# Other tie rules for TensorE in a list scheduler, with the ranks searched anew

## The chip, the cores and the metric

The kernel runs on one core of one Trainium2 chip. The metric is the device time of one execution in microseconds; several executions are timed and the median is given.

## The reference, cut to what matters

32 sequences of 256 tokens with 256 features pass through four layers, all in float32:

```python
out = silu(scale * layer_norm(x) + shift) @ W_in + b_in          # layer 0, norm over the whole sequence
x   = silu(scale * layer_norm(out) + shift) @ W_out + b_out + x
x   = ln(x) * (1 + scale) + shift                                 # layer 1: attention with a bias and a mask
s   = q @ k.T / sqrt(16) + attention_bias                         # 16 heads of 16
x   = x + softmax(where(mask, -inf, s)) @ v @ Wo + bo
x   = x + gelu2((ln(x) * g2 + beta2) @ W1 + b1) @ W2 + b2         # 256 -> 1024 -> 256
x   = max(x + dt * (stencils of x), 0)                            # layer 2: gradients along both axes
h   = layer_norm(x)                                               # layer 3: causal attention, exact gelu
x1  = x + softmax(causal(q @ k.T / sqrt(16))) @ v @ Wo + bo
x2  = x1 + gelu(layer_norm(x1) @ W1 + b1) @ W2 + b2
return x + g * (x2 - x)
```

The batches do not depend on each other; within a batch each layer needs the one before.

## The kernel before, in words

The kernel does not issue its instructions as the program text has them. Every engine is wrapped by a recorder (`Order.engine`, `Order.record`), which notes each operation with its operands, an estimate of its length and its dependences. The three generators `layer_0`, `layer_1` and `layers_23` describe one batch each. The function `trace` runs through a generator and gives each of its steps a rank, which is a wished-for time: batch times `PERIOD`, plus the layer's `START`, plus an `EDGE` for single early and late batches, plus a `SHIFT` for single steps. `PACE` stretches a layer's steps. So several batches lie on top of each other: while layer 3 of one batch runs, layer 1 of the next and layer 0 of a later one run between its operations.

`Order.arrange` then walks through time as a list scheduler. Whenever an engine is free by its own book-keeping, it takes from the operations that are ready the one with the lowest rank. `Order.emit` issues everything in the order of the start times found (line 382 is the one call through which all of it passes, so nearly all rows of the profile name L382; one tells groups apart by their tiles). The order on each engine is thus fixed when the program is built. On the chip the engines run it in order and wait for each other by semaphores.

A TensorE unit is a group of matmuls recorded together. There are three array shapes:

- scores (tile `sc`): 32 rows by 128 columns, four heads beside each other, out of `k_t` and `nq0` or `nq1`;
- values (tile `mm`, out of `pt` and `L1v` or `L3v`): 128 rows by 32 columns;
- everything else is full-size, 128 by 128. It is of two kinds: transposes (tiles `tr`, and `mm` with `ident`), which take one pass, and float32 matmuls, which take two passes. The profile counts passes.

In attention, a scores group of four heads goes to VectorE, which adds the bias and finds the minimum (`pr`, `mn`), then to ScalarE, which takes the exponential in place (`pr`). TensorE transposes the result (`tr`), VectorE and ScalarE copy it to SBUF in turns (`pt`), and the values follow. `wide`, the inverse sums spread by GpSimd, is transposed too and multiplied in. The feed-forward tiles are `h_t`, `L1w` or `L3w` and `hid`; the stencil's are `gd`, `b0f` and `rows_t`; normed rows are `t`.

PSUM has eight banks, all of one tag. `CAPS` says how many of them scores (`sc`), transposed probabilities (`tr`) and other results (`mm`) may hold at once. `EARLIER` lets these kinds go ahead of their rank by so much.

What the change is about stands in the choice of TensorE's next unit, in `arrange`:

```python
if e == "pe" and units[u][2][0]["length"][1] != shape:
    rank += self.STAY
    if units[u][2][0]["length"][1] != (P, P):
        rank -= self.PAIR if shape != (P, P) else 0.0
    elif units[u][2][0]["length"][3] == 2:
        rank += self.FRESH
```

`shape` is the shape that the array has now. A unit of another shape has its rank raised by `STAY` (5.0). If the array has a small shape and the candidate has the other small one, `PAIR` is taken off. If the candidate is a full-size matmul of two passes, `FRESH` is put on; a full-size transpose (one pass) gets neither. Ranks are in the scheduler's own microseconds.

The DMA loads (`nb`, a quarter of a megabyte of attention bias each, `x`, `mask`) are all issued from SyncE's queue in an order that the same scheduler sets.

Of the kernel before, what the change touches and what calls it, by code (L numbers as in the profile page):

```python
# [38 lines left out]

PERIOD = 86.0
START = (-61.8, 0.0, 116.9)
PACE = (1.55, 1.23, 1.08)
EDGE = {(0, 0): 14.4, (0, 1): -5.0, (0, 2): 5.8, (1, 0): -19.0, (1, 1): -3.8, (1, 2): -0.2, (2, 0): -27.1, (2, 1): -2.0, (2, 2): -1.1, (3, 0): 12.3, (3, 1): 0.4, (3, 2): 0.3, (4, 0): 5.2, (4, 1): 2.3, (4, 2): 0.6, (27, 0): -1.1, (27, 1): -1.0, (27, 2): 0.5, (28, 0): 1.7, (28, 1): -0.3, (28, 2): -2.0, (29, 0): 2.1, (29, 1): -0.1, (29, 2): -2.1, (30, 0): -11.1, (30, 1): 5.7, (30, 2): -4.5, (31, 0): -16.9, (31, 1): 1.9, (31, 2): 15.4}
SHIFT = (
    {0: -93.0, 1: -33.6, 2: -27.5, 3: -32.8, 4: -14.7, 5: -56.4, 6: -42.3, 7: -28.3, 8: 23.1},
    {0: -9.7, 1: -80.2, 2: -10.3, 3: -1.7, 4: 2.7, 5: 8.8, 7: -7.0, 8: 14.7, 9: -90.2, 11: 7.3,
     12: 21.2, 13: -0.4, 14: 4.0, 15: -1.3, 16: 11.4, 17: 5.1, 19: 4.8, 20: 10.4, 21: 46.1, 22: 16.4,
     23: -8.7, 24: -13.1, 25: -30.4, 26: -2.4, 27: -90.0, 28: 8.3, 29: -134.0, 30: -0.4, 31: -13.2,  # L50
     32: -34.6, 33: 0.8, 34: -0.3, 35: 7.7, 36: -2.9, 37: -8.0},
    {0: -1.1, 1: -32.9, 2: -9.3, 3: 27.2, 4: 23.9, 5: -25.6, 6: -48.6, 7: -36.4, 8: -12.9, 9: 6.6,
     11: 3.0, 12: 15.4, 13: -32.5, 15: -6.5, 16: 20.0, 17: -2.0, 18: 6.6, 19: -0.5, 20: 0.4, 21: -82.2,
     23: 9.0, 24: 7.5, 25: 0.1, 26: -11.0, 27: -38.3, 28: 12.2, 29: 7.0, 30: 30.4, 31: 3.6, 32: -8.7,
     33: -46.1, 34: 4.4, 35: 2.3, 36: -58.5, 37: -16.3, 38: -59.7, 39: 18.0, 40: -15.2, 41: 12.6},
    {0: -24.5, 1: -13.3, 2: 6.7, 3: -84.2, 4: 42.8},
)
NORM = 8.0
LAND = 3.0
# [5 lines left out]
class Order:  # L65
# [13 lines left out]
    APART = 120.0  # L79
    SLACK = 50.0  # L80
    SEEN = {(32, P): 165.0, (P, 32): -16.0, (P, P): 165.0}
    CAPS = {"sc": 8, "tr": 7, "mm": 7}
    EARLIER = {"sc": 29.6, "mm": -2.0, "tr": 6.2}
    STAY = 5.0
    FRESH = 1.0
    PAIR = 0.0
    PORT = 0.05
    TABLES = {AF.Sin: 0, AF.Tanh: 1, AF.Exp: 1, AF.Gelu: 2}
    TABLE = 1300.0
# [127 lines left out]
    def arrange(self):  # L217
# [5 lines left out]
        turns = defaultdict(list)  # L223
        room = dict(self.CAPS)
        first = {}
        for u, (engine, rank, xs) in enumerate(units):
# [6 lines left out]
            for t in {t.name: t for x in xs for t in x["tiles"]}.values():  # L233
                f = first.setdefault(t.name, u)
                if f == u:
                    room[t.tag] = t.bufs or t.tag_meta.bufs
                    count[t.tag] += 1
                    if t.source_name in self.CAPS:
                        count[t.source_name] += 1
# [10 lines left out]
        for u, (engine, rank, xs) in enumerate(units):  # L250
            name = next((t.source_name for x in xs for t in x["tiles"] if t.source_name in self.CAPS), "")
            ranks.append((rank - (self.EARLIER.get(name, 0.0) if engine == "pe" else 0.0), u))
        for us in turns.values():
# [27 lines left out]
        while todo:  # L281
# [6 lines left out]
            for e in self.ENGINES:  # L288
# [6 lines left out]
                for k, heap in ready[e].items():  # L295
# [5 lines left out]
# [6 lines that stand above are left out]
                    if k[1]:  # L307
# [123 lines left out]
def kernel(ctx: ExitStack, tc: tile.TileContext, io, out, n_batch=B):  # L431
# [89 lines left out]
    def turned_vectors(tag, names, eng):  # L521
        vectors, n_rows = {}, 0
        for name in names:
            n = io[name].shape[0] // P
            vectors[name] = slice(n_rows, n_rows + n)
            n_rows += n
        as_rows = sb.tile([n_rows, P], F32, tag="nq0", name="as_rows")
        for name, at in vectors.items():
            eng.dma_start(as_rows[at], io[name].rearrange("(c p) -> c p", p=P))
        pm = mm_tile([P, n_rows])  # L530
        pe.transpose(pm, as_rows, ident[0:n_rows, 0:n_rows])
        cols = ctile(tag, [P, n_rows])
        dve.tensor_copy(cols, pm)
        return cols, {name: cols[:, at] for name, at in vectors.items()}
# [116 lines left out]
    sync.dma_start(parity, io["c_parity"])  # L651
    order.now = START[0] + 5.0
    _, more = turned_vectors(
# [501 lines left out]
    def trace(n, gen, layer, start, pace):  # L1155
        i = 0
        while True:
            order.now = start + SHIFT[layer].get(i, 0.0)
            step = next(gen, None)
            if step is None:  # L1160
                break
            start += step * pace
            i += 1

    trace(3 * n_batch, loads(), 3, START[1] + 25.0, 1.0)
    res = {}
    for b in range(n_batch):
        for i, layer in enumerate((layer_0, layer_1, layers_23)):
            trace(3 * b + i, layer(b, res), i, b * PERIOD + START[i] + EDGE.get((b, i), 0.0), PACE[i])
    with tc.manual_schedule():  # L1170
# [34 lines left out]
```

## Time and profile before

| | us |
|---|---|
| median of 3 runs (2664.05 to 2667.85) | 2665.15 |
| the profiled execution, its own time | 2665.54 |
| its span, first to last instruction | 2663.7 |
| TensorE busy | 2600.2 |
| VectorE busy | 2122.1 |
| ScalarE busy | 1920.1 |
| GpSimd busy | 1565.0 |

The profile was taken in one execution; its span is 1.8 us shorter than its time. A TensorE row's duration reaches from its start to its modelled end, and one overlaps the next, so what a matmul occupies is read from its start to the start of the next. Rows of the timeline are merged: the first column is the start of the first instruction, the second the time to the end of the last, and x8 is the number of passes. In the rows of the waits, the numbers are the microseconds in total, how often, and the longest. The row PEclk is the clock that TensorE was granted, in tenths of full speed, in 40 equal slices of the span.

### The profile page before, as it was taken

The page shows a single profiled execution, that of the slowest core. Times are in us where ns is not written, and L with a number is a line of the kernel's source. Part 1 is how long each engine was busy: PE and PEld are TensorE (multiplying, and loading weights), DVE is VectorE, ACT ScalarE, POOL GpSimd, SP SyncE. Part 2 cuts the span into 40 slices and gives each one's busy share as a digit, 9 for nine tenths or more (in the row PEclk, how much of TensorE's full clock was granted, in tenths as well). Part 3 has the DMA queues.
Part 4 walks back from the last instruction along what each step waited for, and adds up shares of the span by engine and source line. Part 5 has one row for each costly group of instructions (what it writes and reads, how often), then busy time and mean ns, then how long its engine had stood idle before and what let it go on. Part 6 is the DMA issues. An engine that isn't in the chain of part 4 may idle for free.

```text
span 2663.7 us, 60400 instructions
## 1 busy us (share of the span) xinstructions
PE 2600.2 (98%) x20462; PEld 2118.4 (80%) x20462; DVE 2122.1 (80%) x7627; ACT 1920.1 (72%) x6120; POOL 1565.0 (59%) x1960
## 2 busy tenths in 40 slices
PE   5999999999999999999999999999999999999997
PEld 4777888888888888888888888888888888888775
DVE  5887888878878877878878878877878887887853
ACT  2677777877777877777777777877777877777854
POOL 3865676555676555576555677555576555676420
PEclk7999999999999999999999999999999999999998
DMA  7321122212122212122212122212122211122100
GB/s 243 110 60 59 42 73 69 70 49 66 45 70 70 70 49 66 46 70 69 70 49 65 43 73 70 69 49 66 46 69 69 70 57 57 42 69 64 45 5 9
DMA packets 177064, 169.69 MB, mean 64 GB/s; under 512 B 19514, under 2 KB 175220, under 8 KB 176756
## 3 DMA queue, kind: packets, MB, share of 16 engines
q1 hardware_dynamic: 176720, 165.82, 20.2%
q8 instruction: 163, 2.67, 0.4%
q14 instruction: 145, 1.19, 0.1%
q10 hardware_dynamic: 36, 0.01, 0.0%
HBM read 157.40 MB, written 8.39 MB: 62 GB/s over the span
## 4 chain that ended last, share of the span: by engine, by line
PE 91%; DVE 3%; ACT 2%; DMA 1%; POOL 1%; issue 1%; SPq 0%; ACTq 0%; POOLq 0%; DVEq 0%
PE mm L382 68%; PE tr L382 14%; PE sc L382 9%; DVE pr L382 1%; ACT hid L382 1%; ACT pr L382 1%; DMA x<-in_x_dram 1%; POOL nb L382 0%; DMA nb<-in_fside_Bx16xSxS_dram 0%; DVE pt L382 0%; ACT L382 0%; POOL rstd L382 0%; DVE gd L382 0%; DMA L1wo<-in_L_cond_Wo_dram 0%; DVE st L382 0%
## 5 line engine op out<-in xcount | busy, mean ns | idle before, releaser
L382 ACT ACTIVATE pr<-pr,mn 128x256 f32<-128x256 f32 (+1 forms) x2048 | 966.9, 478 | 93.0 <-DVE mn L382 91.8
L382 POOL TENSOR_TENSOR nb<-mask_f,nb 128x512 f32<-128x512 f32 x512 | 693.3, 1378 | 114.7 <-DMA nb<-in_fside_Bx16xSxS_dram 101.9
L382 PE MATMUL tr<-ident,pr 128*128 128x128 f32 x3584 | 508.5, 276 | 5.4 <-ACT pr L382 1.8
L382 PEld LDWEIGHTS tr<-ident,pr 128*128 128x128 f32 x3584 | 419.5, 143 | 85.8 <-ACT pr L382 29.1
L382 DVE CUSTOM_DVE_ANT_0 pr<-sc,nb 128x256 f32<-128x256 f32 x1024 | 388.0, 414 | 25.3 <-POOL nb L382 14.0
L382 ACT ACTIVATION_READ_ACCUMULATOR pr<-pr,mn 128x1 f32 x2048 | 398.0, 194 | 0.0
L382 DVE COPY pt<-tr 128x512 f32<-128x512 f32 (+1 forms) x512 | 311.3, 615 | 72.9 <-PE tr L382 72.3
L382 POOL TENSOR_SCALAR hid<-hid 128x256 f32<-128x256 f32 x256 | 100.0, 405 | 433.4 <-ACT hid L382 433.1
L382 DVE CUSTOM_DVE_ANT_0 pr<-sc,causal 128x128 f32<-128x128 f32 (+1 forms) x1024 | 299.3, 352 | 38.5 <-PE sc L382 37.2
L382 PE MATMUL sc<-k_t,nq 32*128 32x256 f32 (+1 forms) x4096 | 269.5, 375 | 0.1
L382 ACT COPY pt<-tr 128x512 f32<-128x512 f32 (+1 forms) x512 | 261.4, 526 | 10.9 <-PE tr L382 6.0
L382 PE MATMUL mm<-L3w,hid 128*128 128x256 f32 x1024 | 241.5, 385 | 10.1 <-ACT hid L382 10.0
L382 PE MATMUL mm<-h_t,L3w 128*128 128x256 f32 x1024 | 247.6, 382 | 1.5 <-DVE h_t L382 1.4
L382 PE MATMUL mm<-h_t,L1w 128*128 128x256 f32 x1024 | 248.9, 381 | 0.0
L382 PE MATMUL mm<-L1w,hid 128*128 128x256 f32 x1024 | 239.0, 380 | 0.1
L382 PEld LDWEIGHTS sc<-k_t,nq 32*128 32x128 f32 x4096 | 163.3, 185 | 73.0 <-issue 25.7
L382 PEld LDWEIGHTS mm<-L3w,hid 128*128 128x128 f32 x1024 | 190.6, 193 | 35.1 <-ACT hid L382 11.9
L382 POOL COPY wide<-rs 128x256 f32<-128x256 f32 x128 | 53.3, 416 | 281.3 <-DVE rs L382 131.8
L382 PEld LDWEIGHTS mm<-L1w,hid 128*128 128x128 f32 x1024 | 186.6, 190 | 23.3 <-issue 1.2
L382 PEld LDWEIGHTS mm<-h_t,L3w 128*128 128x128 f32 x1024 | 184.2, 191 | 22.9 <-DVE h_t L382 2.5
L382 PEld LDWEIGHTS mm<-h_t,L1w 128*128 128x128 f32 x1024 | 183.7, 190 | 23.3 <-issue 1.8
L382 ACT ACTIVATE t<-x,shift,rstd 128x256 f32<-128x256 f32 x128 | 67.2, 590 | 148.8 <-DVE shift L382 148.8
(173 smaller groups left out, 4997.7 us busy)
## 6 DMA issues: line engine op xcount, KB each, us to landing
nb<-in_fside_Bx16xSxS_dram SPq DMA_DIRECT2D x512, 256.0 KB
x<-in_x_dram SPq DMA_DIRECT2D x32, 256.0 KB
out_dram<-d SPq DMA_DIRECT2D x32, 256.0 KB
mask<-in_mask_Bx1xSxS_bk_dram SPq DMA_DIRECT2D x32, 64.0 KB
L1w<-in_L_cond_W_dram SPq DMA_DIRECT2D x2, 1024.0 KB
L3w<-in_L_cond_W_dram SPq DMA_DIRECT2D x2, 1024.0 KB
l0w<-in_L_cond_W_dram SPq DMA_DIRECT2D x1, 1024.0 KB
g_b<-in_L_cond_B_grid_dram SPq DMA_DIRECT2D x3, 256.0 KB
```

The source lines that it names most:

```text
L382: call(*args, **kwargs)
```

## The change

Only constants change. `FRESH` goes from 1.0 to 16.0, and `PAIR` from 0.0 to 2.0. So behind a small shape a transpose goes ahead of a two-pass matmul unless its rank is 16 later, and a small group of the other shape is favoured by 2 among those that change the shape. Two bank caps move by one: `tr` may hold 8 and `mm` 6. The tables of ranks were searched together with these values, so they differ nearly everywhere, for the first and last batches most. Since the order of every engine follows from the scheduler, all engines' orders change somewhat, and SyncE's loads too; the instructions themselves are the same.

```diff
-PERIOD = 86.0
-START = (-61.8, 0.0, 116.9)
-PACE = (1.55, 1.23, 1.08)
-EDGE = {(0, 0): 14.4, (0, 1): -5.0, (0, 2): 5.8, (1, 0): -19.0, ...
+PERIOD = 85.9
+START = (-61.4, 0.0, 116.2)
+PACE = (1.47, 1.23, 1.08)
+EDGE = {(0, 0): -157.4, (0, 1): -5.7, (0, 2): 1.4, (1, 0): -49.3, ...
...
-    CAPS = {"sc": 8, "tr": 7, "mm": 7}
-    EARLIER = {"sc": 29.6, "mm": -2.0, "tr": 6.2}
+    CAPS = {"sc": 8, "tr": 8, "mm": 6}
+    EARLIER = {"sc": 28.0, "mm": -3.0, "tr": 6.3}
     STAY = 5.0
-    FRESH = 1.0
-    PAIR = 0.0
+    FRESH = 16.0
+    PAIR = 2.0
```

The entries of `SHIFT`, one per step of a layer, are replaced in the same manner.

## The prediction

> **What bounds the kernel now.** I read the page's busy shares first, then its chain, then TensorE's waits, then the timeline.
>
> ```profile
> PE 2600.2 (98%) x20462; PEld 2118.4 (80%) x20462; DVE 2122.1 (80%) x7627; ACT 1920.1 (72%) x6120; POOL 1565.0 (59%) x1960
> ...
> PEclk7999999999999999999999999999999999999998
> ...
> PE 91%; DVE 3%; ACT 2%; DMA 1%; POOL 1%; issue 1%; SPq 0%; ACTq 0%; POOLq 0%; DVEq 0%
> ```
>
> TensorE is busy for 98% of the span and is 91% of the chain; its clock is full in all but the first and last slices. Only TensorE's own work, and its 63.5 us of idle time (2663.7 - 2600.2), can change the end. TensorE's timeline puts 34.2 us of that idle in the first 100 us, 17.5 us after 2500 us, 5.6 us behind the last matmul, and nearly none between: two waits of 1.0 us, at 1320 and 1401. The chain repeats every 79.7 us per batch. So the middle is pure TensorE work, and what a TensorE instruction occupies there counts in full.
>
> What a change of tile shape costs is in TensorE's timeline. Columns: start, duration, what, how many passes.
>
> ```profile
> 1346.59 1.89 PE L382 MATMUL mm<-h_t,L3wk 128*128 128x256 f32 x8
> 1348.32 1.03 PE L382 MATMUL mm<-L3wv,h_t 128*128 128x256 f32 x4
> 1349.27 0.94 PE L382 MATMUL sc<-k_t,nq 32*128 32x128 f32 x16
> 1350.14 1.13 PE L382 MATMUL mm<-L3wv,h_t 128*128 128x256 f32 x4
> 1351.20 0.94 PE L382 MATMUL sc<-k_t,nq 32*128 32x128 f32 x16
> 1352.07 0.66 PE L382 MATMUL mm<-ident,t 128*128 128x128 f32 x4
> 1352.56 0.49 PE L382 MATMUL tr<-ident,pr 128*128 128x128 f32 x3
> ...
> 1366.05 1.15 PE L382 MATMUL sc<-k_t,nq 32*128 32x256 f32 x16
> 1367.13 1.51 PE L382 MATMUL mm<-pt,L3v 128*32 128x256 f32 x32
> 1368.57 0.87 PE L382 MATMUL tr<-ident,pr 128*128 128x128 f32 x6
> ...
> 1375.71 2.35 PE L382 MATMUL tr<-ident,pr 128*128 128x128 f32 x20
> 1377.89 3.62 PE L382 MATMUL mm<-L1w,hid 128*128 128x256 f32 x16
> ```
>
> Read from start to start. Eight full-size passes take 1.73 us, 0.216 each. The four at 1348.32, with scores next, take 0.95, not 0.86: **entering** a small shape costs 0.09. The four at 1350.14 lie between two score groups and take 1.06: **leaving into a matmul** costs 0.10 more. The four transposes at 1352.07 take 0.49 against 4 x 0.109: **leaving into a transpose** costs 0.056. Scores followed directly by values take 1.08, as before anything else, and the values take 1.44, as they do behind a full-size one: **small directly behind small** pays no entry. Medians over the trace: entry 93.5 ns, exit to a matmul 104 ns, exit to a transpose 56 ns.
>
> **The change part by part.** No instruction is added or removed: both orders hold 12606 TensorE instructions. The constants move only ranks, so I counted the boundaries in the two built orders.
>
> - Entries into a small shape from a full-size one: 327 before, 305 after. 22 x 93.5 ns = 2.06 us less.
> - Exits into a two-pass matmul: 96 to 46. 50 x 104 ns = 5.20 us less.
> - Exits into a transpose: 229 to 256. 27 x 56 ns = 1.51 us more.
> - Sum: 5.7 us less TensorE work. In one steady batch it is one entry less, two matmul exits less and one transpose exit more: 0.25 us of 79.7, 22 times (5.4 us). As a check, slots by kind plus these costs give 79.42 us per batch before; the trace has 79.71.
>
> **What could eat it in the middle.** Moving a group brings its operands due earlier or later. Links from TensorE through other engines back to TensorE keep their room in the steady batch: scores to transposes at least 4.5 us apart (3.3 before). Shorter are the last transpose before an L3 values group, 2.37 us ahead instead of the 2.94 that the trace ran without a wait (a pt copy takes 0.53 to 0.62, and the transpose's result about 0.27 more), rows_t to the norm's transposes (12.1 from 14.3; the chain needs 7.6, below) and layer 0's output to its norm (8.6 from 10.2). I charge nothing: 0 from one side; from the other 0.5 us per batch, 11 us. On POOL one nb subtraction (1.38 us) now stands between the two rstd steps behind the output projection, but that link grows from 7.86 to 8.73. SyncE's queue has the same loads in a batch, one nb load earlier past the mask; nb loads are covered, since DMA is busy a fifth of the time.
>
> **The tail.** Here the order changes most. After the last pass of layer 1's feed-forward, before has 51.3 us of work in a chain of 88.7 (2575.0 to 2663.7); after has 56.5 us. The 5.3 us more that lie inside the chain come off what precedes it. How long is the chain then?
>
> ```profile
> 2585.23 0.60 PE L382 MATMUL mm<-ident,rows_t 128*128 128x128 f32 x4
> 2589.55 8.26 PE L382 MATMUL mm<-L3w,hid 128*128 128x256 f32 x24 [3.71 <-ACT hid L382]
> 2597.64 0.60 PE L382 MATMUL mm<-ident,t 128*128 128x128 f32 x4
> ```
>
> The last batch's t was ready at 2593.4 (ScalarE's timeline), but its transposes queued until 2597.64 behind 24 passes of the batch before, at half clock after the 3.7 us idle. After, those transposes come directly behind rows_t: 4.2 us sooner, and 1.2 sooner ahead of them (four matmuls gone, stencil less late). The price: 7.6 us idle with nothing to fill it, so the 20 passes of Q, K and V (4.3 us) run partly at half clock, 3.3 us more. The previous batch's first feed-forward, 6.9 us, now lies in pieces between the attention's transposes: before took 26.9 us for 15.3 us of such work, after has 22.6 us in it; I add 1.5. Its second one fills the 3.7 us idle behind the last output projection, delays t by 1.5, but keeps the clock (FF1 took 8.73 instead of 6.9): zero. Sum -0.6, so the tail is worth 5.9 at best; the terms are estimates of 2 to 3 us each, and I take **4**, between 9 and -4.
>
> **The head.** Batch 1's layer 0 (l_win, two mean matmuls) now goes ahead of batch 0's Q. From before's rows that puts Q some 2.2 us later than 52.0, but takes about 2 us of TensorE and 5 us of VectorE work out of the attention behind it, where before idles 7 us and has one more half-clock stretch. I take 0.5 us gained, between 5 and -4.
>
> **Sum.** 2663.7 - 5.7 - 4 - 0.5 = 2653.5; with the 1.8 us around the span 2655.3 against the profiled execution's 2665.54, which lies 0.4 above the median of the runs (2665.15). I give 2655.
>
> **A rule that speaks against it.** The Trainium skill, "TensorE: Matmul & The Clock Gate", Part 4 (PE-mode transpose), says that a transpose takes about 275 ns in a kernel and does not count as activity for the clock in the way a matmul does. Transposes first would then make duller stretches behind small tiles: one window of the page's 3.4 us at half clock in a batch costs 1.7 us, 37 us over 22 batches. The trace disagrees: 20 transposes in a row at 1375.71 start 109 ns apart (their 276 ns is duration, overlapped), and the clock stays full through every such run in the middle. I go by the row.
>
> **Rivals.**
>
> *The ends give it back (chance 0.22).* The unfilled 7.6 us idle halves the clock for the whole attention behind it (as it did in stretches from 2616 to 2629), and the head's delay is not recovered: +6 on the forecast, 2661. For it: the clock did drop after every such idle. Against it: feed-forward matmuls now lie there.
>
> *Slower: VectorE loses the port (0.15).*
>
> ```profile
> 1238.20 0.68 DVE L382 TENSOR_TENSOR gd<-gd,a0f 128x512 f32<-128x512 f32 x1
> ...
> 1318.16 1.80 DVE L382 TENSOR_TENSOR gd<-gd,a0f 128x512 f32<-128x512 f32 x1
> ```
>
> The same instruction took 1.80 us when POOL's nb subtraction had started 0.01 us earlier (1318.15), and 0.68 when nb came later (1238.98). The stencil matmul then waited 1.0 us, and that batch lasted 80.98 us, not 79.71; so the next. It is a race of some 0.2 us, lost in 2 of 22 batches. The Trainium skill, "SBUF — State Buffer", Who interferes with whom, says that issue order decides and the loser blocks for the whole instruction: by it a small shift flips every batch, by the row 2 in 22. The new order keeps this place's sequence on TensorE, VectorE and POOL, so I keep 2. Lost in all, it costs 20 x 1.27 = 25 us: 2680. From 12 more lost batches the kernel is slower by over 0.2%.
>
> *The values' last copy is late (0.08).* 0.5 us per batch: 2666, no change.
>
> **How the numbers follow.** Forecast 0.55, with its own range 2648 to 2661. A measurement can tell about 0.2% from no change: 2659.8 to 2670.5 is "same". Faster: nearly all of the forecast and some of the first rival, 0.62; same 0.24; slower 0.14. The range for 8 in 10 takes the forecast's low end, the first rival and the copies' case: 2647 to 2668.
>
> **What would show it.** Right: boundaries in TensorE's timeline counted as above; a batch of about 79.45 us; no waits in the middle; busy TensorE some 6 us lower; t's transposes directly behind rows_t at the end after 7 to 8 us idle. Wrong: waits of 0.3 us or more repeated every batch in front of values or stencil (gd at 1.8 us), a clock below full in the middle slices, or from the last layer-1 feed-forward pass to the end much over 89 us.

## The result, and the profile after

| | before | after |
|---|---|---|
| median, us (20 runs each) | 2665.37 | 2669.17 |
| span of the profiled execution, us | 2663.7 | 2667.5 |
| up to batch 0's first L3wq matmul | 150.2 | 150.3 |
| batches 0 to 2 | 236.4 | 235.6 |
| batches 3 to 24, the 22 steady ones | 1756.7 | 1768.4 |
| the five behind them, 25 to 29 | 393.8 | 406.8 |
| the last two, to the end | 126.7 | 106.4 |

The ratio of after to before is 1.0014, with an interval of 1.0008 to 1.0021: slower by a little, where 2655 was forecast. (A batch is counted from its first L3wq matmul to that of the next.) The middle lost 11.7 us where 5.4 were to be gained; from batch 25 on it was 7.3 us faster.

First the page of after: busy time by engine, the granted clock, the chain by engine. (ScalarE's count has fallen by two: the program as it ran has 63 table loads, before had 65. All other instructions are the same in number.)

```profile
PE 2596.2 (97%) x20462; PEld 2123.4 (80%) x20462; DVE 2152.6 (81%) x7627; ACT 1927.2 (72%) x6118; POOL 1558.9 (58%) x1960
...
PEclk7999999999999999999999999999999999999999
...
PE 82%; ACT 7%; DVE 6%; POOL 2%; DMA 2%; issue 1%; SPq 0%; DVEq 0%; POOLq 0%; ACTq 0%
```

The clock is at nine tenths or more in all slices but the first, so no boundary has become dearer by the clock. But the chain that ended last lies on TensorE for 82% only, not 91%, and ScalarE has grown from 2% to 7%: TensorE waits for something more often. Its waits name it (total, how often, longest), first in after, then the same row in before:

```profile
PE tr L382 <- ACT pr L382: 13.7, 49, 1.2
```

```profile
PE tr L382 <- ACT pr L382: 1.8, 6, 0.5
```

The 6 waits have become 49, two in each steady batch. TensorE's timeline shows where, in a steady batch of after whose first L3wq matmul starts at 1109.56:

```profile
1117.62 0.94 PE L382 MATMUL sc<-k_t,nq 32*128 32x128 f32 x16
1118.49 0.55 PE L382 MATMUL tr<-ident,pr 128*128 128x128 f32 x3
1119.38 0.33 PE L382 MATMUL tr<-ident,pr 128*128 128x128 f32 x1 [0.35 <-ACT pr L382]
1119.88 0.77 PE L382 MATMUL tr<-ident,pr 128*128 128x128 f32 x5 [0.16 <-ACT pr L382]
1120.48 0.60 PE L382 MATMUL mm<-ident,t 128*128 128x128 f32 x4
```

Nine transposes directly behind layer 3's second scores group, as the new ties want it. They take 1.99 us from start to start (1118.49 to 1120.48) where nine in a row and one exit take 1.04: **0.95 us lost in each batch**. They wait for exponentials, so the next view is ScalarE's timeline of the same stretch, first in after:

```profile
1111.12 0.63 ACT L382 ACTIVATE th<-y 128x512 f32<-128x512 f32 x1 [2.52 <-DVE y L382]
1113.21 0.84 ACT L382 ACTIVATE k_t<-mm,cols 128x256 f32<-128x256 f32 x2 [1.46 <-PE mm L382]
1114.14 1.09 ACT L382 ACTIVATE t<-xm,shift,rstd 128x256 f32<-128x256 f32 x2
1115.25 1.28 ACT L382 ACT_TABLE_LOAD   x1
1116.55 0.40 ACT L382 ACTIVATE pr<-pr,mn 128x128 f32<-128x128 f32 x1
```

and in before (the batch starts at 1104.47):

```profile
1104.76 0.63 ACT L382 ACTIVATE th<-y 128x512 f32<-128x512 f32 x1 [1.24 <-DVE y L382]
1105.30 1.08 ACT L382 ACTIVATE t<-xm,shift,rstd 128x256 f32<-128x256 f32 x2
1108.12 0.84 ACT L382 ACTIVATE k_t<-mm,cols 128x256 f32<-128x256 f32 x2 [1.75 <-PE mm L382]
1108.98 1.28 ACT L382 ACT_TABLE_LOAD   x1
1110.28 0.40 ACT L382 ACTIVATE pr<-pr,mn 128x128 f32<-128x128 f32 x1
```

The same five rows stand in another order. `k_t` starts 3.65 us into the batch in both. In before, layer 1's second norm (`t<-xm`, 1.08 us) ran ahead of it, in time in which ScalarE idled. In after it stands behind it, between `k_t` and the first exponential, because the shift that it needs now lies behind `nq` in VectorE's queue. It came 0.17 us into the batch in before and comes 4.34 us into it in after (a row of each):

```profile
1104.64 0.33 DVE L382 TENSOR_SCALAR shift<-mv,rstd 128x1 f32<-128x1 f32 x2
```

```profile
1113.90 0.33 DVE L382 TENSOR_SCALAR shift<-mv,rstd 128x1 f32<-128x1 f32 x2
```

So the first exponential starts 6.99 us into the batch, not 5.81, and all those behind it are 1.2 us later. The table load, 1.28 us, is in that stretch in both.

### The profile page after: what moved, and what is told of

It reads as the page before. It is cut to its first block, busy times and chain, and to the rows that moved or that the text cites. A ratio compares the mean times of both kernels' runs of the same rounds, so it can differ in the third digit from the quotient of the medians.

```text
span 2667.5 us, 60293 instructions
## 1 busy us (share of the span) xinstructions
PE 2596.2 (97%) x20462; PEld 2123.4 (80%) x20462; DVE 2152.6 (81%) x7627; ACT 1927.2 (72%) x6118; POOL 1558.9 (58%) x1960
## 4 chain that ended last, share of the span: by engine, by line
PE 82%; ACT 7%; DVE 6%; POOL 2%; DMA 2%; issue 1%; SPq 0%; DVEq 0%; POOLq 0%; ACTq 0%
PE mm L382 61%; PE tr L382 14%; PE sc L382 7%; ACT pr L382 3%; DVE nq L382 2%; ACT L382 1%; ACT t L382 1%; POOL nb L382 1%; DVE pr L382 1%; DVE dd L382 1%; DMA nb<-in_fside_Bx16xSxS_dram 1%; DVE th L382 1%; DMA x<-in_x_dram 1%; ACT L3v L382 0%; ACT hid L382 0%
## 5 line engine op out<-in xcount | busy, mean ns | idle before, releaser
L382 PEld LDWEIGHTS tr<-ident,pr 128*128 128x128 f32 x3584 | 412.6, 142 | 110.3 <-ACT pr L382 40.4
L382 DVE COPY pt<-tr 128x384 f32<-128x384 f32 (+1 forms) x512 | 308.7, 613 | 28.6 <-PE tr L382 26.0
L382 PE MATMUL mm<-h_t,L1w 128*128 128x256 f32 x1024 | 244.3, 380 | 0.4 <-DVE h_t L382 0.4
L382 PE MATMUL mm<-h_t,L3w 128*128 128x256 f32 x1024 | 239.2, 380 | 0.6 <-DVE h_t L382 0.3
L382 DVE DVE_READ_ACCUMULATOR2_ANT mn<- 128x1 f32 x2048 | 167.9, 82 | 0.0
```

What stands on the lines that cost most here:

```text
L382: call(*args, **kwargs)
```

## The experiments

**Theory A**: what stands in ScalarE's queue between `k_t` and layer 3's first exponential sets the steady batch, through the exponentials that the nine transposes read; take 1 us of it away, and the 0.95 us go. **Rivals**: B, that TensorE's own order is at fault, which puts too little work between scores and transposes; C, that taking this wait away does not bring the time back, since it moves on; later D, that the strong tie puts the transposes too early whatever stands on ScalarE; and E, that each microsecond off that queue shortens the batch. All times below are medians of at least four runs, beside before on the same chip; spans and batches are from each kernel's profile.

### table_early: the table drawn forward

```diff
         for x in sorted(xs, key=lambda x: x["start"]):
+            if x.get("mark") == "k3":
+                early()
...
-        order.emit()
+        order.emit(lambda: nc.scalar.activation(spare, mhalf[:, 0:1], AF.Exp))
```

A one-column exponential of a constant is issued on ScalarE ahead of each layer-3 `k_t`. Nothing else moves.

> The changed kernel plus one exponential of a single column on ScalarE ahead of each layer-3 k_t, whose result nobody reads: the table load of 1.28 us then falls into ScalarE's idle time of 1.46 us ahead of k_t. No other instruction moves. Theory A: first exponential at about 5.7 us behind the batch's first Q matmul instead of 7.0, no wait in front of the transposes, 2648 (2645 to 2652). Theory B: 2669. Theory C: 2658 to 2666.

Measured: 2643.55 us, ratio to before 0.9921 (0.9907 to 0.9935). ScalarE's timeline of it, in a batch that starts at 1098.28:

```profile
1100.51 1.28 ACT L1177 ACT_TABLE_LOAD   x1
1101.80 0.20 ACT L1177 ACTIVATE spare<-mhalf 128x1 f32<-128x1 f32 x1
1101.94 0.84 ACT L385 ACTIVATE k_t<-mm,cols 128x256 f32<-128x256 f32 x2
1102.88 1.09 ACT L385 ACTIVATE t<-xm,shift,rstd 128x256 f32<-128x256 f32 x2
1103.98 0.40 ACT L385 ACTIVATE pr<-pr,mn 128x128 f32<-128x128 f32 x1
```

The load now lies in the 1.46 us that ScalarE idled ahead of `k_t`, and `k_t` starts at 3.66 us as it did. The first exponential comes at 5.70 us, and the nine transposes run without a gap, 1.04 us from their start to that of the next row (TensorE's timeline):

```profile
1107.22 1.20 PE L385 MATMUL tr<-ident,pr 128*128 128x128 f32 x9
1108.26 0.60 PE L385 MATMUL mm<-ident,t 128*128 128x128 f32 x4
```

The batch is 79.35 us, the middle 1748.1: 20.3 us less than after, 22 times 0.92. This is theory A's mechanism, and the fastest kernel of the study. It is 1.5 us faster than the range that A gave. The middle alone does not account for that: in the profiled execution 3.5 us of the gain lie ahead of the first L3wq matmul (146.8 us, from 150.3), where nothing had been meant to change, and 4.2 behind batch 24.

### before_table_early: the same in before

> The control: the kernel before with the same early exponential. Its TensorE does not wait at that place, so theory A expects no change, 2665 (2663 to 2667). A gain of several us would say that the kernel before was held by the table load too.

Measured: 2666.41 us, ratio 1.0001 (0.9992 to 1.0009), batch 79.71 as in before. The place of the table load costs before nothing, so the gain of the run above is not one that any kernel would have had.

### norm_ahead: the norm back to where before had it

```diff
+            refs = nqs if x["method"] == "tensor_scalar" else ks
+            before = [r["start"] for r in refs if x["start"] - 3000.0 < r["start"] < x["start"]]
...
+                x["start"] = max(max(before) - 1.0, floor) + 1e-3 * (1 + i % 4)
```

The two shift instructions go ahead of `nq` on VectorE, the two norm activations ahead of `k_t` on ScalarE. TensorE's order is untouched.

> The changed kernel with its TensorE order untouched; only layer 1's second norm is moved in the queues: its two shift steps on VectorE stand ahead of nq, its two normalising steps on ScalarE ahead of k_t, so that the table load and the first exponentials of layer 3 come 1.1 to 1.2 us sooner. Theory A (the norm slipped behind k_t on ScalarE, so the table load and the exponentials are late for the transposes, 0.95 us in each steady batch): the wait in front of the transposes goes, a batch takes 79.35 to 79.5 us, the time is 2669 - 21 = 2648 (2645 to 2652). Theory B (transposes directly behind scores are exposed by their place on TensorE, whatever ScalarE does ahead of it): 80.3 us per batch, 2669. Theory C (the wait is only moved, since VectorE or ScalarE are behind anyway): 2658 to 2666.

Measured: 2647.92 us, ratio 0.9934 (0.9921 to 0.9947), batch 79.35, middle 1747.1. ScalarE's row of the norm, then TensorE's of the nine transposes:

```profile
1105.49 1.09 ACT L395 ACTIVATE t<-xm,shift,rstd 128x256 f32<-128x256 f32 x2 [0.19 <-DVE shift L395]
```

```profile
1112.02 1.20 PE L395 MATMUL tr<-ident,pr 128*128 128x128 f32 x9
```

Another instruction of 1.09 us taken out of the same place gives the same batch. With TensorE's order unchanged and the wait gone in both runs, B falls as the cause, and so does C for these two repairs: the time came back. The 4.4 us between the medians of this run and the one above are not of the middle: in the profiled executions the first L3wq matmul came at 152.6 us here and at 146.8 there.

### matmul_first: other work in front of the transposes

```diff
+            before = [r["start"] for r in trs if x["start"] - 4000.0 < r["start"] < x["start"]]
+            if before:
+                x["start"] = min(before) - 1.0 + 1e-3 * (i % 8)
```

Layer 1's four Q matmuls (1.73 us), which stood some way behind the nine transposes, are issued ahead of them; ScalarE's queue stays as it is in after.

> The changed kernel with one step of its tie rule undone by hand: layer 1's four Q matmuls stand ahead of the nine transposes behind layer 3's second scores group, where the change has them behind; ScalarE's queue stays as it is, the table load too. It costs one more exit into a matmul in a batch (48 ns, 1.1 us in all). Theory A and theory B both expect that the transposes, 1.8 us later, find their rows ready: 79.4 us per batch, 2649 (2646 to 2654). If the wait stays near 0.95 us, both fall.

Measured: 2681.48 us, ratio 1.0064 (1.005 to 1.0077), batch 80.79. The expected gain did not come. The nine transposes no longer wait, but TensorE's waits have a new first row, and the old one is still there at another place:

```profile
PE mm L392 <- DVE h_t L392: 7.2, 23, 0.4
PE tr L392 <- ACT pr L392: 5.9, 26, 1.2
```

The first wait has a plain reason. In after, the four Q matmuls stand between the transposes of layer 1's `t` (1120.48) and the first feed-forward matmul that reads `h_t` (1122.97), and cover the time in which VectorE makes `h_t`. Here nothing covers it:

```profile
1125.66 0.66 PE L392 MATMUL mm<-ident,t 128*128 128x128 f32 x4
1126.22 0.52 PE L392 MATMUL tr<-ident,pr 128*128 128x128 f32 x3
1127.05 1.97 PE L392 MATMUL mm<-h_t,L1w 128*128 128x256 f32 x8 [0.31 <-DVE h_t L392]
```

`h_t` also comes 1 us later in the batch, and behind it in VectorE's queue stand operations that the next exponentials read; the second wait, 19 us into the batch, fits that, but was not taken apart. So this edit closed one link and opened others. It does not tell A from B, since neither foresaw that.

### before_delayed: the delay put into before

```diff
             call(*args, **kwargs)
+            if x["mark"] == "k3":
+                late()
...
+        def late():
+            for i in range(8):
+                nc.scalar.activation(spare, mhalf[:, 0:1], AF.Identity)
```

> The kernel before, with eight one-column activations put on ScalarE directly behind each of layer 3's k_t, that is ahead of the table load and the exponentials; all other orders stay. Such an activation took about 0.14 us from start to start behind the table load of the kernel with the early table, so some 1.1 us in all, as much as layer 1's second norm (1.09 us). In before the fewest spare time between an exponential's end and the transpose that reads it, in this stretch, is about 0.3 us (third quarter: exponential ends at 8.88 us behind the batch's first L3wq matmul, transpose due at 9.2). Theory A (what stands in ScalarE's queue ahead of layer 3's first exponentials sets the steady batch): the batch grows from 79.71 us by 1.1 - 0.3, 0.8 us, to 80.5, and the time from 2666 by 22 to 29 times 0.8 to about 2686 (2680 to 2692), waits of transposes for ACT pr. Rival (the order of after waits for a reason of its own, and before's queues have room): under 2670.

Measured: 2708.69 us, ratio 1.0161 (1.0147 to 1.0175): twice the expected loss. The waits are where A expects them:

```profile
PE tr L383 <- ACT pr L383: 16.9, 85, 0.8
```

ScalarE's timeline says why the loss is so large (the batch starts at 1120.26):

```profile
1123.92 0.84 ACT L383 ACTIVATE k_t<-mm,cols 128x256 f32<-128x256 f32 x2 [1.75 <-PE mm L383]
1124.64 1.85 ACT L1179 ACTIVATE spare<-mhalf 128x1 f32<-128x1 f32 x8
1126.51 1.28 ACT L383 ACT_TABLE_LOAD   x1
```

The eight took 1.85 us, not 1.1, and the load starts 1.74 us later in the batch than in before (6.25, from 4.51). The batch grew from 79.71 to 81.31, by 1.60: all of the delay but 0.14. So the dose was mis-sized, and the rival falls: before's queues have next to no room at this place. If all beyond the room goes into the batch one for one, before had 0.14 us to spare; one dose cannot show more than that.

### norm_and_table_early: both repairs

> After with both repairs at once: layer 1's second norm (and its shift on VectorE) ahead of nq and k_t, and a one-column exponential ahead of k_t that draws the table load forward. Theory A says that the time hangs on a wait which either repair takes away whole, so the second adds nothing: batch 79.35 us, 2641 to 2648. Rival E (every microsecond taken from ScalarE's queue there shortens the batch, so the gains add): batch 78.4, about 2622.

Measured: 2673.93 us, ratio 1.0029 (1.0018 to 1.0041): neither number. ScalarE's timeline (batch from 1109.12), then TensorE's:

```profile
1111.52 1.09 ACT L397 ACTIVATE t<-xm,shift,rstd 128x256 f32<-128x256 f32 x2 [0.19 <-DVE shift L397]
1112.63 1.28 ACT L1195 ACT_TABLE_LOAD   x1
1113.92 0.20 ACT L1195 ACTIVATE spare<-mhalf 128x1 f32<-128x1 f32 x1
1114.03 0.82 ACT L397 ACTIVATE k_t<-mm,cols 128x256 f32<-128x256 f32 x2
```

```profile
1114.54 0.94 PE L397 MATMUL sc<-k_t,nq 32*128 32x128 f32 x16 [0.94 <-ACT k_t L397]
```

The idle time ahead of `k_t` is 1.46 us. Norm, load and spare exponential need 2.5. So `k_t` started 4.91 us into the batch, 1.26 late, the scores waited 0.94, and the batch is 80.36: 1.01 above that with either repair alone. I had counted what the repairs take out of one place and not what they put into the one ahead of it, which is the prediction's mistake over again. So the run tests neither A nor E as it was meant to. What speaks against E are the two single repairs: the first exponential starts at 5.70 us in table_early and at 5.81 in norm_ahead (1103.09 to 1108.90), and the batch is 79.35 in both.

### ranks_weak_tie: after's ranks with a third of the tie

```diff
-    FRESH = 16.0
+    FRESH = 5.0
```

> The ranks of after with a tie of 5 in place of 16. The order of the first 22 us of a batch is that of after on TensorE and ScalarE: nine transposes behind the scores, the norm behind k_t. With the prices of the prediction TensorE has 1.2 us more work than in after, all at the ends. Theory A: the same wait, 0.95 us in each steady batch; batch 80.3, about 2670 (2667 to 2673). Rival D (the ties put the transposes too early): with a tie a third as strong the wait goes, batch 79.35, about 2650.

Measured: 2667.74 us, ratio 1.0008 (1.0001 to 1.0015), batch 80.30, 45 waits for `pr`. With the ranks of after a tie of 5 builds the same first 22 us of a batch as one of 16, and the wait is the same. So the tie's strength between 5 and 16 does not matter here. Since the transposes stand at the same place, the run says nothing on whether that place is too early; norm_ahead, with a tie of 16 and no wait, does, and D falls by it.

### ties_alone: before's ranks with after's ties

```diff
-    FRESH = 1.0
-    PAIR = 0.0
+    FRESH = 16.0
+    PAIR = 2.0
```

> The ranks of before with the two tie values of after (16 and 2), so the ties alone. The order that comes out has the same nine transposes directly behind layer 3's second scores group, due 8.9 us into the batch as in after, but on ScalarE nothing stands between k_t and the table load (layer 1's second norm is elsewhere). With the prices of the prediction its TensorE work is 1.9 us less than before's, in a pattern of three batches of 78.9, 79.5 and 79.6 us. Theory A (the norm and the table load in front of the exponentials, which came with the new ranks): no wait at these nine transposes, batch 79.5 us on average, about 2662 (2656 to 2668). Rival D (transposes directly behind scores wait whatever stands on ScalarE, so the ties cost the time): batch 80.3, about 2682. Other links of this order, which was not searched for, can cost more under either.

Measured: 2713.85 us, ratio 1.0181 (1.0167 to 1.0195); batches of 82.1, 82.1 and 80.6 us in turn. At the disputed place A was right (TensorE's timeline):

```profile
1135.18 0.94 PE L382 MATMUL sc<-k_t,nq 32*128 32x128 f32 x16
1136.05 1.20 PE L382 MATMUL tr<-ident,pr 128*128 128x128 f32 x9
1137.09 1.89 PE L382 MATMUL mm<-h_t,L1w 128*128 128x256 f32 x8
```

The nine transposes follow the scores 1.04 us apart from what is next, without a wait, since no norm stands on ScalarE between `k_t` and the load. But the number was wrong, as the last sentence of the expectation allowed: the batches are some 2.3 us longer on average than the 79.5 counted. TensorE's other waits of 0.15 us or more, ended by `hid`, `dev`, `gd`, `t`, `pt` and `mn`, come to 14.2 us from 400 to 2100 us, that is 0.7 us a batch; where the rest goes is open. One of these waits is the prediction's port race. VectorE's `gd<-gd,a0f` from 400 to 2400 us (minimum, median and maximum in ns):

```profile
L382 DVE TENSOR_TENSOR gd<-gd,a0f x24: 650/1082/1764, 450.7 to 2326.6; 128x512 f32<-128x512 f32 x24
```

It is over 1 us in two batches out of three, and the stencil matmul waits. So the ties without the search cost 47 us, and with the searched ranks and the moved caps the time is back at 2669. The norm's new place came with the ranks or the caps, not with the ties. The new ranks with the old ties, and the caps alone, were not run, so what each of them is worth stays open.

## Why the prediction was wrong, point by point

**The boundaries: right, and a little too small.** Entries and exits cost in after what they cost in before: in TensorE's timeline of after, four full-size passes with scores next take 0.95 us (1113.01 to 1113.96), as in before; the four behind those scores (1114.83 to 1115.80) take 0.97, that is 0.10 more than four without a boundary. With the wait gone the batch is 79.35 us, against 79.45 forecast and 79.71 before: 0.36 us less, where 0.25 were counted from boundaries. Where the other 0.11 comes from is open.

**The middle: this step failed.** The prediction said that links "keep their room in the steady batch: scores to transposes at least 4.5 us apart (3.3 before)", and "I charge nothing". The distance on TensorE had grown, as it said. What fills it had grown more. It compared places on TensorE and did not add up what stands in the queue of the engine in between: `k_t` done at 4.5 us, the norm 1.09, the load 1.30 up to the first exponential, then 3.2 us from there to the end of the third pair of exponentials, for transposes that are due 9.4 us into the batch. That sum is 10.1; the transpose in question starts at 10.3 (1119.88), 0.9 us late. All terms of the sum but the new place of the norm stand in the trace of before; the place stands in the built order of ScalarE. The loss, 0.95 us in each of 22 batches (20.3 us by table_early), is twice the upper bound that was set for this step, 0.5 us a batch, which had been taken from other links. So the sum of the middle was -5.4 where -8.6 and +20.3 were right. (Of the 8.6, some 2.5 us are not of the boundaries: before loses the port race in two of these batches, 80.98 us each instead of 79.71, and after's order in none.)

**The tail: right in sign, too small.** The waiting time was foreseen to 0.3 us (rows of TensorE in after):

```profile
2596.64 0.66 PE L382 MATMUL mm<-ident,rows_t 128*128 128x128 f32 x4 [0.66 <-DVE rows_t L382]
2604.62 2.25 PE L382 MATMUL mm<-ident,t 128*128 128x128 f32 x8 [7.33 <-ACT t L382]
2606.66 3.19 PE L382 MATMUL mm<-h_t,L3wq 128*128 128x256 f32 x8
```

From the last layer-1 feed-forward pass to the end it is 79.4 us (2588.15 to 2667.5), from 88.7; 88.1 was forecast. By stretches: up to t's transposes -6.2 (-5.4 forecast); from there to the first scores +1.2 (+3.3); the attention with its output projection -2.5 (+1.5); the rest -1.9 (0). The sign of the third is what was missed. The tables of the windows give the time behind each engine's name in order (TensorE, weight loads, VectorE, ScalarE, GpSimd, with the count of instructions), then the granted clock, the share of the DMA engines and what they moved. Of after, the stretch behind the idle time, the attention with its projection, and the two halves of the last feed-forward:

```profile
2604.00:2609.50 5.50, 4.88 (x16) 3.63 (x17) 2.38 (x7) 2.12 (x4) 3.38 (x4) 0.52 0.01 3
2612.40:2636.90 24.50, 24.05 (x225) 17.56 (x224) 14.32 (x77) 23.20 (x87) 0.80 (x2) 1.00 0.00 1
2645.50:2652.50 7.00, 7.00 (x33) 5.89 (x31) 1.44 (x2) 2.40 (x6) 0.00 (x0) 1.00 0.11 37
2655.40:2662.60 7.20, 7.15 (x32) 6.00 (x32) 0.00 (x0) 0.00 (x0) 0.00 (x0) 1.00 0.00 0
```

and of before, the last three of these:

```profile
2604.20:2631.10 26.90, 24.33 (x193) 15.34 (x192) 13.95 (x76) 19.98 (x78) 0.80 (x2) 0.81 0.01 2
2636.40:2645.10 8.70, 8.65 (x32) 7.11 (x32) 0.45 (x1) 2.40 (x6) 1.26 (x1) 0.81 0.00 0
2649.30:2658.10 8.80, 8.77 (x32) 7.17 (x32) 0.00 (x0) 0.00 (x0) 0.00 (x0) 0.81 0.00 0
```

After its long idle TensorE ran at 0.52 for five microseconds and then at full clock to the end, with 225 instructions in 24.5 us, where before did 193 in 26.9 at 0.81. That feed-forward pieces between the attention's transposes keep the clock up is argued from these rows; it was not tried by an experiment. Counted with the 5.3 us of moved work, these stretches gain 14.6 us; what arrived from batch 25 on is 7.3 in after and 11.4 in table_early. The 4.2 between the last two go with the same repair, and most of them lie in batch 25 (87.05 us in after, 84.18 in table_early), where after waits for `pr` (0.3 us), `h_t` (0.3) and `ctx_t` (1.2) and table_early for none of them; how the first leads to the others was not taken apart. Where the other 3.2 went is open.

**The head: the number fits, which may be luck.** -0.7 us up to batch 3, -0.5 forecast. But builds that share after's order of TensorE there had their first L3wq between 146.8 and 152.6 us, so a difference of this size says little.

**The rivals.** The ends did not give it back. The port race did not decide after: in the 22 batches of its middle `gd` was long in none, against two in before. The copies' case (`pt` to the values) did not show: from 400 to 2100 us TensorE has two waits for `pt`, of 0.6 and 0.5 us, and neither is in front of values. None of the rivals named ScalarE's queue. The rule on transposes and the clock played no part: with more transposes behind small tiles, the clock stayed full through the middle, as the row had it. That is less than the prediction's "the trace disagrees": the runs of 20 transposes that recur in every batch last 2.2 us, and what a longer one does to the clock is not shown here.

## What to carry to other kernels

When an order changes, a link between two engines is not judged by the distance of its ends. Write down, for each engine that it passes, all that now stands in the queue between, table loads included, and add it up to a time of arrival against the time at which it is due. And before moving an instruction ahead of another, compare its length with the idle time that is there: in this kernel 1.46 us had room for one repair, and the second cost as much as the first had gained.

## What the runs showed of the hardware that was not expected

- **The table load comes in front of the exponential, not of the Tanh.** The scheduler's list `TABLES` puts Tanh and Exp into one set and so charges 1.3 us at the Tanh that follows a Gelu. On the chip `th` ran without a load, and the load came behind `k_t`, with the first exponential. So the scheduler's book-keeping has the load in ScalarE's idle time ahead of `k_t`, where table_early then put it, and does not see the 1.3 us behind `k_t`. That would explain why such an order looked good to it; no kernel with a corrected list was built. The Trainium skill, "ScalarE: Activation LUTs", Table sets: the hidden batching unit, has exponential and Tanh in one set too, but a function can be in several; what Gelu's set holds is shown here only by the missing load.
- **The load took 1.31 us in all**, from the end of the norm (5.68 us into the batch) to the start of the exponential (6.99), and about as much in every kernel here. The same page, What ACT_TABLE_LOAD costs, gives some 2.66 us for each switch, a drain included; the time between these rows has no room for such a drain, and the measurement stands.
- **One-column activations in a row start 0.23 us apart** (eight in 1.85 us); the 0.14 from one to a `k_t` activation (1101.80 to 1101.94 in table_early), from which the dose was estimated, was no guide.
- **The port race repeats.** `gd` took 1.8 us in batches 14 and 15 of before, and in the same two, and no other steady ones, of before_table_early and of before_delayed. In the steady part it looks fixed by the order of the instructions, not left to chance; each kernel was profiled once. (In batch 0 it took 1.7 us in before alone.)
